# The first set of head tiles in a pool of its own, in a decoder kernel of twelve layers on one core

## The chip, the cores and the metric

The kernel runs on one core of a Trainium2 chip. A core has five engines that work side by side, each through a queue of its own: TensorE (PE, with its weight loads listed as PEld), VectorE (DVE), ScalarE (ACT), GpSimd (POOL) and SyncE (SP), which here only issues DMAs. The metric is the time of one execution on the device in microseconds. Before the change it was 1789.06 us, the median of three runs (1786.39, 1789.06 and 1797.75).

## The reference

The input `x` has 8 batches of 256 tokens of width 128, the context 8 batches of 512 tokens. Four decoder blocks follow, each with a self-attention, a cross-attention and a feed-forward layer, each added to `x` after a normalisation:

```python
x = x + _L0_attn_ref(_layernorm(x), ...)
...
x = x + _L1_attn_ref(_layernorm(x), ...)            # rotary, over the batch axis
x = x + _L1_xattn_ref(_layernorm(x), ctx_1024, ...) # one head
x = x + _L1_ffn_ref(_layernorm(x), ...)
x = x + _L2_attn_ref(_layernorm(x), ...)            # Fenwick mask, 16 heads
x = x + _L2_xattn_ref(_layernorm(x), ctx_1024, ...) # 16 heads
...
```

The layers around the change are the single-head cross-attention of block 1 and the two attentions of block 2:

```python
def _L1_xattn_ref(input_tensor, context, Wq, bq, Wk, bk, Wv, bv):
    q = jnp.einsum('bld,ed->ble', input_tensor, Wq) + bq
    k = jnp.einsum('bld,ed->ble', context, Wk) + bk
    v = jnp.einsum('bld,ed->ble', context, Wv) + bv
    scores = jnp.einsum('bqd,bkd->bqk', q, k) / q.shape[-1] ** 0.5
    return jnp.einsum('bqk,bkd->bqd', jax.nn.softmax(scores, axis=-1), v)
...
def _L2_xattn_ref(q, kv, ...):
    qh = (q @ Wq.T + bq).reshape(B, Lq, 16, 8)
    kh = (kv @ Wk.T + bk).reshape(B, Lkv, 16, 8)
    vh = (kv @ Wv.T + bv).reshape(B, Lkv, 16, 8)
    attn = jax.nn.softmax(jnp.einsum('bqhd,bkhd->bhqk', qh, kh) / 8 ** 0.5, axis=-1)
    return jnp.einsum('bhqk,bkhd->bqhd', attn, vh).reshape(B, Lq, 128) @ Wo.T + bo
```

The change leaves what is computed as it is.

## The kernel before

The activations stay in the core's memory throughout: `E.x` holds the 8 batches, `xt` their normalised transposes. The kernel falls into parts. First L0_attn and L0_xattn run woven together. Then the middle part (`_middle`, L1185) runs L0_ffn, L1_attn, L1_xattn, L1_ffn and L2_attn. Then come L2_xattn, L2_ffn and block 3.

**Head attention.** L0_xattn, L2_xattn, L3_attn and L3_xattn are computed by one function, `_heads_attention`, with tiles that the class `_Heads` (L345) holds in a pool named "hd". There are two sets of them, i = 0 and 1, used by turns: `mh_v` (2,672 B per partition), `mh_k` (16,384 B) and `mh_q` (16,384 B). Products of heads of width 8 use rows of `mh_k` and `mh_q` of which some must hold zeros and some ones, and `mh_v` has columns of ones, so each set is filled once before its first use. The function `fills` (L363) yields four copies per set on ScalarE, all by line L368 from a column of zeros or ones: the upper 64 rows of `mh_k`, two rows of `mh_k`, `mh_q`, and `mh_v`.

**When the tiles are made.** At the start of the kernel `_Heads` is made for L0_xattn. The middle part needs the space, so "hd" is closed before it (L1737) and `_Heads` is made anew towards its end: in `_middle`, after `scope.close()` (L1230), `E.beginning(then)` makes it through `heads()` (L1635), issues the first four fills, begins the layer (the bias row `mh_row` from `mh_bvt` and `mh_bps`), projects the keys and values of batch 0 (L422, L441) and starts to spread the keys by DMA. Then `fa(0, 1)` (L1237) runs the Fenwick attention over the first two batches (four half blocks, tiles `fa_`). The second `next(begun)` (L1239) projects the queries of batch 0 (`mh_qps`), spreads them by DMA (L438), and issues the remaining four fills, those of set 1. The rest of L2_attn and L1_ffn then run as a guest among the steps of L2_xattn.

**The layers before it.** `_middle` runs groups of two batches through L0_ffn (tiles `moe_`), the rotary L1_attn (`ra_`) and L1_xattn (`xa_`), staggered. At the end stand `ra(3)`, `xa(2)` and `xa(3)` (L1227 to L1229). L1_xattn ends in the additions of L1030. `ra` reads its projections from `ra_qkv` (24,576 B per partition); the products over it are those of L946 and L965, on VectorE and on GpSimd.

**Space.** Pools are stacks on a left and a right side of the memory. On the right side of the middle part lie, from the bottom: "moe" (two buffers of 4,096 B and two of 2,048 B per partition), "moe_c" (512 B), "ra1" (`ra_qkv`), then the smaller buffers of `ra_`, `xa_` and `rk_`. All are closed by `scope.close()`, after which the head pools are opened on the same side, from the bottom. A new pool's tile waits for those who last used the memory under it.

**Order.** The program is written out in full, and a scheduler that lays out the instructions of each engine may place one ahead of others that are written earlier, by the inputs that it expects to be ready. Steps of the head layers on TensorE keep their written order (`keep_in_program_order`, L459). Each engine then takes its instructions strictly as laid out. The lines that the prediction follows are these: L957 and L1008 (exponentials of `ra_` and `xa_`), L1025 (`xa_et`), L1117 (`fa_v`), L1131 (exponential of `fa_`), L1152 (`fa_ot`), L215 (`xt`) and L425 (`mh_kf`, `mh_qf`) on ScalarE; L1113 (`fa_kvps`) and L459 on TensorE.

Of the kernel before, what the change touches and what calls it, by code (L numbers as in the profile page):

```python
# [344 lines left out]
class _Heads:  # L345
# [4 lines left out]

    def __init__(self, E, ctx):
        self.E, nc = E, E.nc
        one = ctx.enter_context(E.tc.tile_pool(name="hd", bufs=1, side="right"))
        self.g = ctx.enter_context(E.tc.tile_pool(name="hd_g", bufs=2, space=PSUM, side="right"))
        self.one = one
        self.q, self.k, self.v = [], [], []
        for i in range(2):
            self.v.append(one.tile([P, SK // P, H * VW + 32 - VW], F32, name=f"mh_v{i}"))
            self.k.append(one.tile([P, H // 2, SK], F32R, name=f"mh_k{i}"))
            self.q.append(one.tile([P, H, S], F32R, name=f"mh_q{i}"))  # L360
        self.made = 0
# [1414 lines left out]
```

## Time and profile before

The profiled execution is one of the kernel on the chip. Its device time was 1792.07 us, of which 1790.2 lie between its first and last instruction.

| | before |
|---|---|
| median of three runs | 1789.06 us |
| profiled execution, device time | 1792.07 us |
| its span | 1790.2 us |
| mean granted TensorE clock | 0.917 |
| TensorE busy | 1475.6 us (82%) |
| VectorE busy | 1149.6 us (64%) |
| ScalarE busy | 882.0 us (49%) |
| GpSimd busy | 495.5 us (28%) |
| fills by L368 (8 long, of 3.60 us, for `mh_k`; 4 of 3.61 for `mh_q`; 4 of 0.76 for `mh_v`) | 14.4 + 14.4 + 14.4 + 3.1 us |

Eight of these sixteen fills are those of the start; the other eight lie between 862 and 894 us. Times in the timelines are counted from the span's start. A row of a timeline gives the start, the busy time, engine and line, the operation, the tile written and the tiles read, shapes, how many instructions were merged, and in brackets the idle time of the engine just before and what ended it. A share of busy time is an average over stages with different limits, so a stage is read by its own windows.

### The profile page before, as it was taken

Reading aid. Unit: us, or ns where it says so; the run is one execution under the profiler, and the core shown is the slowest. Engines: PE = TensorE matmul, PEld = TensorE weight load, DVE = VectorE, ACT = ScalarE, POOL = GpSimd, SP = SyncE. Lnnn points to the kernel's source line nnn. Section 1 sums busy time; section 2 is a strip of 40 time slices with the busy share of each in tenths; the row PEclk is TensorE's granted clock in tenths of the full one; section 3 lists DMA queues with packets and bytes.
Section 4 is the critical chain, followed back from the end, with each engine's and each line's share of the span. In section 5 each row is a group of like instructions: output and inputs, shape, how many; then the busy total and the mean of one; then the engine's idle time right before and its main releaser. Section 6 shows DMA issues by size and latency. Waiting matters only on the chain. (4 is left out here: it accounts for less than half of the span.)

```text
span 1790.2 us, 29309 instructions
## 1 busy us (share of the span) xinstructions
PE 1475.6 (82%) x10103; PEld 1066.1 (60%) x10141; DVE 1149.6 (64%) x3857; ACT 882.0 (49%) x1830; POOL 495.5 (28%) x987
## 2 busy tenths in 40 slices
PE   5689989999999989786558888878946799799986
PEld 3456677767655556554336666656615677677763
DVE  3567666765636676777457777668565666466656
ACT  7245455555642345322625656547643465455543
POOL 3122222222100121223323334332103433234422
PEclk8799999999999999897769999989965899899999
DMA  4011011104100000000111011111002221112100
GB/s 153 13 36 36 8 33 37 36 21 151 30 1 1 1 1 1 0 1 1 24 38 26 22 37 37 37 37 42 5 10 54 83 67 50 49 50 52 48 1 24
DMA packets 47236, 60.43 MB, mean 34 GB/s; under 512 B 5232, under 2 KB 36976, under 8 KB 46448
## 3 DMA queue, kind: packets, MB, share of 16 engines
q1 hardware_dynamic: 44720, 56.99, 12.0%
q8 instruction: 80, 1.31, 0.3%
q10 hardware_dynamic: 2368, 1.57, 0.3%
q14 instruction: 68, 0.56, 0.1%
HBM read 14.50 MB, written 1.05 MB: 9 GB/s over the span
## 5 line engine op out<-in xcount | busy, mean ns | idle before, releaser
L459 PE MATMUL mh_sps<-mh_k,mh_q 96*128 96x512 f32 (+2 forms) x1024 | 325.1, 400 | 53.2 <-DMA mh_q<-mh_qp 24.1
L459 PE MATMUL mh_bsps<-mh_q,mh_k 128*128 128x256 f32 (+1 forms) x1536 | 354.9, 337 | 7.0 <-ACT mh_e L595 4.1
L595 ACT ACTIVATE mh_e<-mh_bsps 128x512 f32<-128x512 f32 x512 | 281.0, 599 | 119.1 <-PE mh_bsps L459 111.9
L459 PEld LDWEIGHTS mh_bsps<-mh_q,mh_k 128*128 128x128 f32 x1536 | 267.8, 199 | 32.0 <-issue 6.9
L459 PEld LDWEIGHTS mh_sps<-mh_k,mh_q 96*128 96x128 f32 x1024 | 173.7, 204 | 101.0 <-issue 44.0
L522 DVE CUSTOM_DVE_ANT_0 mh_rest<-mh_sps,mask_b 128x512 bf16<-128x512 f32 x256 | 167.1, 684 | 81.2 <-PE mh_sps L459 78.0
L459 PE MATMUL mh_ops<-mh_e,mh_v 128*32 128x256 f32 (+1 forms) x3072 | 195.2, 375 | 1.3 <-DVE mh_nm L522 0.8
L541 DVE TENSOR_REDUCE mh_nm<-mh_sps 128x1 f32<-128x512 f32 x256 | 165.1, 680 | 33.8 <-PE mh_sps L459 33.6
L582 ACT ACTIVATE mh_e<-mh_bsps 128x384 f32<-128x384 f32 x256 | 118.7, 494 | 59.6 <-PE mh_bsps L459 36.2
L459 PEld LDWEIGHTS mh_ops<-mh_e,mh_v 128*32 128x32 f32 x3072 | 94.9, 112 | 67.0 <-issue 6.2
L197 POOL TENSOR_SCALAR ln_rstd<-ln_mv 128x2 f32<-128x2 f32 x96 | 22.0, 229 | 384.3 <-DVE ln_mv L195 384.0
L548 POOL CAST mh_hi<-mh_nm 128x8 fp32r<-128x8 f32 x128 | 25.0, 196 | 343.4 <-DVE mh_nm L522 211.1
L522 DVE CUSTOM_DVE_ANT_0 mh_rest<-mh_sps,causal 128x128 bf16<-128x128 f32 (+1 forms) x256 | 79.4, 352 | 50.5 <-PE mh_sps L459 48.4
L522 DVE CUSTOM_DVE_ANT_0 mh_rest<-mh_sps,km_q 128x128 bf16<-128x128 f32 (+1 forms) x256 | 79.4, 350 | 45.2 <-PE mh_sps L459 43.3
L215 ACT COPY xt<-ln_ps 128x256 f32<-128x256 f32 x96 | 36.0, 375 | 122.7 <-PE ln_ps L462 62.7
L560 ACT CAST mh_m<-mh_mps 8x256 fp32r<-8x256 f32 x128 | 46.2, 361 | 100.6 <-PE mh_mps L462 99.0
L885 ACT ACTIVATE moe_si<-moe_gps 128x512 f32<-128x512 f32 x64 | 38.0, 597 | 106.5 <-PE moe_gps L883 82.8
L628 ACT COPY mh_osb<-mh_ops 128x256 f32<-128x256 f32 x128 | 47.7, 372 | 84.2 <-PE mh_ops L459 84.0
L459 PE MATMUL mh_bsps<-mask_t,ident 128*128 128x512 bf16 x219 | 84.7, 387 | 0.4 <-ACT mh_e L595 0.4
L201 DVE TENSOR_SCALAR ln_z<-x,ln_mv,ln_rstd 128x128 f32<-128x128 f32 x136 | 44.3, 367 | 54.5 <-POOL ln_rstd L198 54.4
L883 PE MATMUL moe_ups<-xt,w_L_ffn 128*128 128x512 f32 x128 | 69.8, 628 | 6.9 <-ACT moe_si L885 4.8
L894 PEld LDWEIGHTS moe_dps<-w_L_ffn,moe_act 128*128 128x128 f32 x512 | 66.1, 204 | 15.7 <-issue 7.8
(360 smaller groups left out, 3089.5 us busy)
## 6 DMA issues: line engine op xcount, KB each, us to landing
mh_k<-mh_kp SPq DMA_DIRECT2D x64, 256.0 KB
mh_q<-mh_qp SPq DMA_DIRECT2D x256, 64.0 KB
mh_k<-mh_kp SPq DMA_DIRECT2D x64, 128.0 KB
w_L_ffn<-in_w_L_ffn SPq DMA_DIRECT2D x2, 1558.0 KB
w_L_attn<-in_w_L_attn SPq DMA_DIRECT2D x2, 1056.0 KB
ctx_t<-in_ctx_t SPq DMA_DIRECT2D x4, 512.0 KB
mh_q<-mh_m ACTq DMA_DIRECT2D x128, 8.0 KB
w_L_ffn<-in_w_L_ffn SPq DMA_DIRECT2D x2, 687.0 KB
```

What stands on the lines that cost most here:

```text
L201: (engine or nc.vector).tensor_scalar(z[:, q, :], E.x[:, 2 * b + q, :], mv[:, q, 0:1], rstd[:, q : q + 1], ALU.subtract, ALU.mult)
L215: E.nc.scalar.copy(E.xt(b), ps.rearrange("p q t -> p (q t)"))
L459: return self.E.tc.keep_in_program_order(self.E.nc.tensor.matmul(*a, **kw))
L522: nc.vector.tensor_tensor_reduce(rest[:, : scores.shape[1]], scores, lowered, -1.0, -FLOOR, ALU.add, ALU.min, accum_out=at)
L541: nc.vector.tensor_reduce(u.nm[:, c, col], ps, AX.X, ALU.max, negate=True)
L560: nc.scalar.copy(m, ps[:8].rearrange("p c q -> p (c q)"))
L582: nc.scalar.activation(e, ps, AF.Exp, scale=scale)
L595: nc.scalar.activation(e, ps, AF.Exp, scale=scale)
L628: nc.scalar.copy(osbs[b][:, u4 % 2, :], ops)
L883: nc.tensor.matmul(ps, W("w13")[:, o : o + P], xt, start=True, stop=True)
L885: nc.scalar.activation(si, pgate, AF.Silu)
L894: nc.tensor.matmul(ps[:, t, :], act[:, c, t * P : t * P + P], W("w2")[:, o : o + P], start=c == 0, stop=c == 1)
```

## The change

The first set of head tiles gets a pool of its own, "hd0", opened ahead of "hd" on the same side, so it takes the lowest 35,440 B per partition. The second set, and the tiles that `self.one` serves later (`mh_bvt`, `mh_row` and the buffers of the projections), stay in "hd", which now begins above.

```diff
     def __init__(self, E, ctx):
         self.E, nc = E, E.nc
+        zero = ctx.enter_context(E.tc.tile_pool(name="hd0", bufs=1, side="right"))
         one = ctx.enter_context(E.tc.tile_pool(name="hd", bufs=1, side="right"))
         self.g = ctx.enter_context(E.tc.tile_pool(name="hd_g", bufs=2, space=PSUM, side="right"))
         self.one = one
         self.q, self.k, self.v = [], [], []
-        for i in range(2):
+        for i, one in enumerate((zero, one)):
             self.v.append(one.tile([P, SK // P, H * VW + 32 - VW], F32, name=f"mh_v{i}"))
             self.k.append(one.tile([P, H // 2, SK], F32R, name=f"mh_k{i}"))
             self.q.append(one.tile([P, H, S], F32R, name=f"mh_q{i}"))
```

From L353 on, the lines of the changed kernel have numbers higher by one.

## The prediction

> **What bounds the kernel now.** I read the page first. TensorE is busy for 82% of a span of 1790.2 us, so time that the kernel loses lies in short stretches where TensorE waits. The chain of waits at the end of the page sits in the last layer and does not reach the change. So I went to the windows of 10 us around the end of the single-head cross-attention (tiles `xa_`) and the first half of the Fenwick attention (`fa_`), which lead into the head attention of L2_xattn (`mh_`).
>
> ```profile
> 840.00:850.00 10.00, 7.44 (x32) 5.33 (x31) 7.51 (x22) 4.08 (x11) 3.23 (x2) 0.84 0.00 0
> ...
> 860.00:870.00 10.00, 6.88 (x34) 5.33 (x32) 5.72 (x20) 7.61 (x5) 1.23 (x3) 0.89 0.00 0
> 870.00:880.00 10.00, 3.64 (x11) 2.88 (x11) 2.37 (x9) 9.96 (x11) 4.09 (x4) 0.62 0.27 70
> ...
> 900.00:910.00 10.00, 2.19 (x6) 1.10 (x6) 1.37 (x5) 0.85 (x2) 2.77 (x5) 0.50 0.12 30
> ```
>
> The columns are the stretch, its length, the busy time (and instructions) of TensorE, its weight loads, VectorE (DVE), ScalarE (ACT) and GpSimd, the granted clock of TensorE and the DMA's share and rate. From 870 to 880 us ScalarE is full, 9.96 of 10 us, while TensorE works 3.64 and VectorE 2.37. The timeline of ScalarE shows with what:
>
> ```profile
> 862.65 3.60 ACT L368 CAST mh_k<-plain 64x4096 fp32r<-64x4096 f32 x1 [2.35 <-DVE x L1030]
> 866.28 0.37 ACT L215 COPY xt<-ln_ps 128x256 f32<-128x256 f32 x1
> 866.66 3.60 ACT L368 CAST mh_k<-plain 2x4096 fp32r<-2x4096 f32 x1
> 870.27 3.60 ACT L368 CAST mh_q<-plain 128x4096 fp32r<-128x4096 f32 x1
> 873.78 0.74 ACT L368 COPY mh_v<-plain 128x668 f32<-128x668 f32 x1
> ...
> 876.27 0.35 ACT L1131 ACTIVATE fa_sc<-fa_sc 128x128 f32<-128x128 f32 x1
> ...
> 884.24 3.60 ACT L368 CAST mh_k<-plain 2x4096 fp32r<-2x4096 f32 x1
> 887.87 0.93 ACT L1117 COPY fa_v<-fa_kvps 128x256 f32<-128x256 f32 x3
> 888.66 3.63 ACT L368 CAST mh_q<-plain 128x4096 fp32r<-128x4096 f32 x1
> ```
>
> Four fills of the first set of head tiles, 3.60 + 3.60 + 3.60 + 0.74 = 11.5 us, wait for the last addition of the `xa_` layer (DVE L1030, 862.21 us). The work of `fa_` stands behind them. Its exponential (L1131) has its input at 870.62 us, when VectorE's L1130 ends, and starts at 876.27. Three of the second set's fills follow between later steps. TensorE's timeline shows who pays:
>
> ```profile
> 875.92 0.47 PE L1182 MATMUL fa_tps<-ident,fa_o 128*128 128x128 f32 x1 [8.39 <-ACT fa_v L1117]
> ...
> 892.89 0.79 PE L1155 MATMUL fa_yps<-w_L_attn,fa_ot 128*128 128x128 f32 x2 [3.79 <-ACT fa_ot L1152]
> ...
> 903.54 1.06 PE L459 MATMUL mh_qps<-xt,w_L_xattn 128*128 128x256 f32 x2
> 912.21 2.35 PE L459 MATMUL mh_sps<-mh_k,mh_q 96*128 96x512 f32 x4 [7.61 <-DMA mh_q<-mh_qp]
> ```
>
> TensorE waits 8.39 and 3.79 us for ScalarE. What then sets the start of the head attention (912.21) is batch 0's way through `fa_` to the query projection `mh_qps` at 903.54, and the spreading of the queries by DMA. The keys are not late: their DMAs are issued at 875.8.
>
> **The change part by part.** Sizes first. From the bottom of the right side lie the MoE buffers (2 x 4,096 + 2 x 2,048 B per partition), 512 B of gate weights and `ra_qkv` (24,576 B): 37,376 B. The new pool holds 2,672 + 16,384 + 16,384 = 35,440 B, so it ends inside `ra_qkv`. In the built order of the changed program its first fill waits for the two last products over `ra_qkv` (L965: VectorE's ends at 829.24 us, GpSimd's at 827.51), not for `xa_`. The second set still waits for the last L1030. No instruction is added or removed on any engine, SP's queue is the same throughout, and outside 825 to 905 us no engine's order changes.
>
> ScalarE's new order puts the first set's fills here: one ahead of two `xa_e`, one ahead of the copy of xt for batch 7, one ahead of another xt copy and `xa_q`, and the short one after `xa_k`. The second set moves up into the freed place, again with `fa_` work between. I walk that order forward from 825 us, each instruction starting when its engine is free and its inputs are there, with durations of the rows: fills 3.60, `xa_e` 0.69, `xa_et` 0.59, `fa_v` copies 0.37 (0.28 apart), a `fa_kvps` matmul 0.44 apart at full clock. The same walk over the old order brings `mh_qps` to 901.1 with matmuls at their shortest spacing and to 904.2 with spacings 1.4 times that; the trace has 903.54. So I carry both.
>
> *To the last addition of `xa_`.* Fill one runs 829.3 to 832.9, so the first `xa_e` slips from 831.6 to 832.9. Fill two runs 834.2 to 837.8: the xt copy slips from 835.7 to 837.8. Fill three runs 838.1 to 841.7: `xa_q` slips from 838.4 to 842.0. But `xa_k` slips only from 841.0 to 842.4, because the `fa_v` copies that stood before it now stand behind, and the second `xa_e` of that batch comes at 846.4 instead of 847.0. ScalarE was idle for 6.39 us before 831.59 and for 2.24 and 1.46 before the two copies; that is the cover. The last L1030 ends up 1.0 us earlier with short matmuls, 0.1 with long ones. If the cover fails, the 3.7 us of `xa_q` are lost.
>
> *From there to the exponential of the third half block.* Before: 876.27 - 862.21 = 14.1 us, four fills and 2.6 us of copies. After: 0.4 to start, a fill 3.6, xt copy 0.3, `mh_kf` and `mh_v` 1.0, two `fa_v` copies with their waits 1.1, a fill 3.6, two copies 0.6, and 0.2: 10.8 us. With long matmuls the `fa_v` copies wait longer, 12.65 (the old order gives 14.2 there). Gain 1.6 to 3.2. Of the 11.5 us of fills only 11.5 - 2 x 3.6 = 4.3 leave this stretch, since the second set moves in.
>
> *From there to `mh_qps`.* Before 903.54 - 876.27 = 27.3. There the second key fill (884.24) held the `fa_v` copies that free the banks of `fa_kvps`, and the query fill held the next exponential until 892.33. After, both fills lie while ScalarE waits for the normalised batch 0 (idle 3.17 before 883.57 now). The last `fa_kvps` follows 9.5 us after the exponential instead of 12.0, and the path is 24.3; with long matmuls 26.0 against 28.05 for the old order. Gain 2.0 to 3.1.
>
> Sum: 1.0 + 3.2 + 3.1 = 7.3 at best, 0.1 + 1.6 + 2.0 = 3.7 at worst. Granted clocks of 0.84 and 0.89 between 840 and 870 lie between the two; the trace's 903.54 is nearer the long matmuls. The middle is 5.5; I take 5. What is late next is the query DMA (905.61 to 912.21), which starts earlier by the same 5 and costs the same; all orders behind it are unchanged, so the 5 us stay.
>
> The clock is the open price. Rows: 0.50 in a window where TensorE worked 2.19 us, 0.62 at 3.64, and 0.89 at 6.88. The new order opens gaps of 2.1 and 2.0 us on TensorE (836.4 to 838.5 and 840.4 to 842.4). In the old order the matmuls up to 841 us ran slow already (`xa_kps` took 1.91 us at 839.09, where `mh_kps` of the same shape took 1.02 at 863.61). The new gaps could keep the next ones slow: two `xa_sps` 1.74, `xa_vps` 0.89 and `xa_tps` 0.44, or 3.1 us more. I count half of a microsecond of it in the 5, since the row of 840 to 850 (0.84) is nearer full clock than half. [...]
>
> **The rivals.**
> - All of the stall goes: 8.39 + 3.79 = 12.2 us. For it: these are the waits on TensorE. Against: the second set's fills move into the place. 1789.06 - 12.2 = 1776.9.
> - The gain is eaten: half clock after the new gaps costs 3.1, or the second set's fills hold the Fenwick block as the first did. Gain 0 to 2, taken as 1: 1788.
> - Slower: the three long fills delay `xa_q` by 3.7 us, the half clock adds 3.1, and the last L1030 comes 6.8 late, at 869.0; the later stretches return 3.6 to 6.3, the low end of which leaves 3.2 lost: 1792.3. It decides from a last L1030 between 865.8 and 868.5 on. Against it: `xa_k` slips only 1.4.
> - No fill moves, because the new pool waits for more than `ra_qkv`: 1789. Against it: the order and its waits.
>
> **How the numbers follow.** The profiled execution took 1792.07 (span 1790.2 and 1.87 around it), 3.0 above the median of 1789.06. 1792.07 - 5 = 1787.1 for such an execution, 1784.1 for the median. Chances: forecast (gain 3 to 8) 0.55, all of the stall 0.10, eaten 0.22, slower 0.10, no move 0.03. Range 1776 to 1793, from the full stall to the slower case; the three runs before spread from 1786.39 to 1797.75, so a median can sit a few us off by itself. 1% is 17.9 us, about what a measurement of this kernel can tell from no change, and no case reaches it: within 1% 0.95, faster 0.02, slower 0.03 for what I have not seen.
>
> **What would show it.** First fill at 829 to 830 us, and its four fills over by about 844. The `xa_e` behind it near 833. Last L1030 within 2 us of 862. One fill, not four, between it and `mh_kf`. TensorE's wait of 8.39 down to about 4 (for `fa_ot`). `mh_qps` near 898.5, and the same 8.7 us from it to `mh_sps`. I am wrong if the last L1030 passes 865.8, if the second set's fills stand in front of `fa_` exponentials for longer than 4 us, or if the granted clock between 835 and 850 falls under 0.7.

## The result and the profile after

The changed kernel took 1781.57 us (median of 11 runs, 1776.44 to 1788.22) against 1790.25 for the kernel before (11 runs beside them, 1786.39 to 1797.75). The medians lie 8.7 us apart. The ratio of the runs beside one another is 0.9956, 95% interval 0.9944 to 0.9967, or 7.9 us faster, between 5.9 and 10.0; that is less than 1%, and I go by it. The prediction said 5 us faster and a range of 1776 to 1793, so range and direction held and the gain was larger than said.

The profiled execution of after has a span of 1783.2 us and a mean granted clock of 0.921. Its times can't be laid over those of before as they stand. The copy of xt at 820.86 us, ahead of which both kernels have the same code, comes at 823.84. Over all twelve profiled executions of this study it lies between 816.1 and 824.6. So every time below is also given from that copy.

Windows of the changed kernel, with the columns of the prediction's first fence (stretch, length, busy time of TensorE, its weight loads, VectorE, ScalarE and GpSimd, granted clock, DMA):

```profile
840.00:850.00 10.00, 7.51 (x28) 4.50 (x29) 6.96 (x25) 9.61 (x17) 0.94 (x2) 0.77 0.00 1
...
860.00:870.00 10.00, 7.13 (x38) 5.28 (x36) 5.55 (x20) 7.43 (x7) 5.01 (x8) 1.00 0.10 25
870.00:880.00 10.00, 4.87 (x14) 3.63 (x15) 6.02 (x18) 7.34 (x9) 5.22 (x6) 0.60 0.35 80
...
890.00:900.00 10.00, 2.86 (x7) 1.48 (x7) 2.67 (x9) 1.11 (x3) 3.74 (x7) 0.50 0.00 0
```

ScalarE is now full between 840 and 850 (9.61 us) instead of between 870 and 880, where it fell from 9.96 to 7.34 while VectorE went from 2.37 to 6.02. ScalarE's timeline in the changed kernel shows where the fills went (all of L369):

```profile
832.30 3.60 ACT L369 CAST mh_k<-plain 64x4096 fp32r<-64x4096 f32 x1 [4.12 <-DVE ra_pv L966]
835.93 0.69 ACT L1009 ACTIVATE xa_e<-xa_sps,xa_nm 128x512 f32<-128x512 f32 x1
...
845.06 0.49 ACT L995 ACTIVATE xa_q<-xa_qps,w_L_xattn 128x256 f32<-128x256 f32 x1
845.43 0.70 ACT L999 ACTIVATE xa_k<-xa_kps,w_L_xattn 128x512 f32<-128x512 f32 x1
...
862.40 3.60 ACT L369 CAST mh_k<-plain 64x4096 fp32r<-64x4096 f32 x1 [3.15 <-DVE x L1031]
...
866.29 0.69 ACT L426 ACTIVATE mh_kf<-mh_kps,w_L_xattn 128x512 f32<-128x512 f32 x1
...
868.26 3.60 ACT L369 CAST mh_k<-plain 2x4096 fp32r<-2x4096 f32 x1
...
872.42 0.32 ACT L1132 ACTIVATE fa_sc<-fa_sc 128x128 f32<-128x128 f32 x1
```

The first fill starts when the rotary products end (`ra_pv`), as forecast. One fill stands between the last addition (`x` L1031) and `mh_kf`, where there were three long ones and a short one. TensorE's timeline in the changed kernel:

```profile
872.95 0.80 PE L1156 MATMUL fa_yps<-w_L_attn,fa_ot 128*128 128x128 f32 x2 [3.74 <-ACT fa_ot L1153]
...
893.11 0.48 PE L1183 MATMUL fa_tps<-ident,fa_o 128*128 128x128 f32 x1 [8.39 <-DVE fa_o L1149]
...
897.74 1.06 PE L460 MATMUL mh_qps<-xt,w_L_xattn 128*128 128x256 f32 x2
906.29 2.34 PE L460 MATMUL mh_sps<-mh_k,mh_q 96*128 96x512 f32 x4 [7.49 <-DMA mh_q<-mh_qp]
```

The wait of 8.39 for ScalarE is gone; the longest wait for ScalarE in this stretch is now 3.74, for `fa_ot`. A wait of 8.39 for VectorE's `fa_o` stands later, where before had 5.31 (at 899.00). The three stretches of the prediction, worked out from these rows and those of before:

| stretch | before | after | gain | predicted |
|---|---|---|---|---|
| xt copy to last addition | 862.21 - 820.86 = 41.35 | 861.96 - 823.84 = 38.12 | 3.23 | 0.1 to 1.0 |
| to the exponential of the third half block | 14.06 | 10.46 | 3.60 | 1.6 to 3.2 |
| to `mh_qps` | 27.27 | 25.32 | 1.95 | 2.0 to 3.1 |
| from `mh_qps` to `mh_sps` | 8.67 | 8.55 | 0.12 | 0 |

Together 8.9 us from the copy to the head attention. The spans differ by 7.0, since after came to the copy 2.98 later and took 1.08 less behind `mh_sps`. The first row is the one to explain: ScalarE does more work there than before, and yet the stretch got shorter.

### The profile page after: what moved, and what is told of

Same layout as the page of the kernel before. It is cut to its first block, busy times and chain, and to the rows that moved or that the text cites. A ratio compares the mean times of both kernels' runs of the same rounds, so it can differ in the third digit from the quotient of the medians.

```text
span 1783.2 us, 29345 instructions
## 1 busy us (share of the span) xinstructions
PE 1471.9 (83%) x10141; PEld 1064.4 (60%) x10141; DVE 1149.2 (64%) x3857; ACT 881.3 (49%) x1830; POOL 495.7 (28%) x987
## 5 line engine op out<-in xcount | busy, mean ns | idle before, releaser
L460 PE MATMUL mh_bsps<-mask_t,ident 128*128 128x512 bf16 x256 | 99.9, 390 | 0.4 <-ACT mh_e L596 0.4
```

The lines of the kernel that those rows point to most:

```text
L460: return self.E.tc.keep_in_program_order(self.E.nc.tensor.matmul(*a, **kw))
```

## The experiments

An edge `issue_after(i)` lays an instruction behind `i` in the order of the same engine; what else moves is the scheduler's answer to it. Ratios are to the kernel before, run beside each. The code shown leaves out the lines that only hand an instruction on or say for which set and layer the edit holds. The first four columns are from one profiled execution of each kernel: last addition counted from the xt copy, from there to the exponential of the third half block, from there to `mh_qps`, and the copy to `mh_sps`.

| kernel | last addition | to exponential | to `mh_qps` | copy to `mh_sps` | ratio (95%) |
|---|---|---|---|---|---|
| before | 41.35 | 14.06 | 27.27 | 91.35 | 1 |
| after | 38.12 | 10.46 | 25.32 | 82.45 | 0.9956 (0.9944 to 0.9967) |
| hold_before | 40.32 | 14.06 | 25.46 | 88.47 | 0.9987 (0.9972 to 1.0001) |
| hold_after | 38.14 | 11.81 | 18.77 | 77.36 | 0.9928 (0.9907 to 0.9950) |
| fa_behind | 40.12 | 22.04 | 19.94 | 90.79 | 1.0003 (0.9993 to 1.0013) |
| fills_late | 41.59 | 17.82 | 21.13 | 89.16 | 0.9987 (0.9972 to 1.0002) |
| rstd_first | 40.97 | 14.06 | 27.26 | 90.94 | 0.9989 (0.9977 to 1.0001) |
| products_last | 38.72 | 16.19 | 27.11 | 90.68 | 1.0006 (0.9995 to 1.0016) |
| add_first | 36.90 | 12.40 | 18.76 | 76.62 | 0.9931 (0.9908 to 0.9954) |
| one_less | 38.81 | 9.82 | 18.76 | 76.01 | 0.9934 (0.9916 to 0.9953) |
| one_more | 39.77 | 14.55 | 19.01 | 81.95 | 0.9968 (0.9949 to 0.9986) |
| all_in | 39.52 | 9.71 | 18.77 | 76.61 | 0.9915 (0.9902 to 0.9928) |

### The fills of the second set, on both kernels

Both kernels with this edit:

```diff
-            for f in fills[4:]:
-                f()
+            with tc.issue_after(E.heads.full.ins):   # the activation that makes mh_qf
+                for f in fills[4:]:
+                    f()
```

On the kernel before:

> The kernel before with the four fills of set 1 laid behind mh_qf, the activation of the queries of batch 0; set 0 waits for the xa_ layer as before. Theory 1 (each long fill of ScalarE that stands among the Fenwick steps costs its 3.6 us, or what is left of it after its cover): stretches up to the exponential of the third half block as before (last L1030 near 862, exponential 14 after it); from there to mh_qps 23 to 25.5 us instead of 27.3; the start of the head attention unchanged relative to mh_qps, since ScalarE idles for about 11 us there; total 2 to 4 us faster than before, 1786 to 1788. Rival (the fills only fill waits that DVE and GpSimd set anyway): that stretch stays at 27 to 27.5, total within 1 us of before.

Measured: the stretch to `mh_qps` took 25.46, within the theory's 23 to 25.5, and the head attention started 2.9 us earlier. The time is 2.3 us lower, but its interval (5.0 lower to 0.2 higher) just takes in no change. TensorE has the order of before in every instruction here, and yet the last addition came at 40.32 instead of 41.35; the granted clock between 850 and 860 was 0.96 in this execution and 0.84 in that of before. So that first number scatters by about 1 us.

On the changed kernel:

> The changed kernel with the four fills of set 1 laid behind mh_qf. Theory 1: the fill of 3.6 us after the last addition and the one before the exponential of the third half block are gone, so the exponential comes 4 to 7 us after the last L1031 instead of 10.5; from there to mh_qps 22 to 25 instead of 25.3; total 3.5 to 9 us faster than the changed kernel, 1773 to 1778. Rival (without the fills TensorE or VectorE bounds the Fenwick steps): 8.5 us or more after the last addition, 25 to mh_qps, total within 2 us of the changed kernel, 1780 to 1783. Last L1031 near 859 under both, since nothing ahead of it moves.

Measured: 1777.85 us, 12.9 faster than before and within the theory's total. By the two ratios it is some 5 us faster than the change alone; their intervals overlap a little (0.9944 to 0.9950), and in the profiled executions the head attention comes 5.1 us earlier. Its parts fell out otherwise: 11.81 to the exponential, where 4 to 7 was said, and 18.77 behind it, where 22 to 25 was said. TensorE's timeline of this kernel shows what sets the pace with the fills gone:

```profile
876.90 0.45 PE L1183 MATMUL fa_tps<-ident,fa_o 128*128 128x128 f32 x1 [3.86 <-DVE fa_o L1147]
...
884.30 0.45 PE L1183 MATMUL fa_tps<-ident,fa_o 128*128 128x128 f32 x1 [5.79 <-DVE fa_o L1149]
```

The long waits are now for VectorE and the GpSimd product ahead of it; the longest for ScalarE is 0.74. VectorE is busy for 7.57 of the 10 us from 860, and the exponential of the third half block is one of several things that it feeds there; that of the fourth follows 6.9 us later (877.01 - 870.13), not 14.2 (886.58 - 872.42 in after). The two stretches together are the safe reading: 30.6 us instead of 35.8.

### The same pools, without the move

```diff
-            for f in fills[:4]:
-                f()
+            with tc.issue_after(E.last_et.ins) if layer == "L2_xattn" else ExitStack():
+                for f in fills[:4]:
+                    f()
```

> The changed kernel with the four fills of set 0 laid on ScalarE behind the last xa_et, so the two pools and their addresses stay, and the move is taken out but for the 2 us by which the fills may start ahead of the last addition. Theory 1: fills from about 860, exponential of the third half block 12 to 14 us after the last L1031, total 1786 to 1790, like before. Rival (pools, addresses or the freed tiles of the second set matter, not the time of the fills): 1781 to 1783, like the changed kernel.

Measured: ratio 0.9987. The two pools and their addresses are those of the changed kernel, and 5.6 of its 7.9 us are gone; what is left is 2.3 (interval 0.4 slower to 5.0 faster). The fills start at 860.75, as soon as the last `xa_et` is over and 5.4 ahead of the addition (866.20), which no longer gates them. The exponential came 17.8 after the addition, not 12 to 14, because five long fills stand ahead of it here, two of them set 1's. So it is the time of the fills that pays, not the pools.

### Why the last addition came earlier

The first idea was TensorE's order, in which before has Fenwick steps between the `xa_ops`. In the kernel before, all of TensorE's Fenwick steps from the first `fa_tps` on were laid behind the last `xa_ops`:

```diff
+    def behind(op):
+        def issue(*a, **kw):
+            with E.tc.issue_after(E.last_ops.ins):
+                return op(*a, **kw)
+        return issue
+    ...
+        E.mm = behind(nc.tensor.matmul)
```

> The kernel before with TensorE's Fenwick steps from the first fa_tps on laid behind the last xa_ops; the fills stay behind the xa_ layer. Theory 2 (the 3.2 us that the changed kernel gains up to the last addition come from the order of TensorE, which had Fenwick steps between the xa_ops): last L1030 at 859 to 860.5 instead of 862.2, then as many us later in the Fenwick part; total 1787 to 1792. Rival (they come from the early fills themselves or from the granted clock): last L1030 at 861.5 to 863 and total 1789 to 1793.

Measured: last addition 40.12 after the copy, 1.2 earlier than in before and 0.2 earlier than in hold_before, which has the old order. By the clock of the trace it lies at 859.91, but the copy came 1.07 earlier too. The total is unchanged. The scheduler's answer also moved GpSimd: its second product then stood ahead of `ln_rstd`, which ended at 858.39. So the run does not weigh TensorE's order by itself, but that order alone, with no more gain than the scatter, does not account for 3.2 us. Next, the chain that ends in the last addition was read on all engines. The kernel before:

```profile
853.87 0.17 DVE L195 BATCH_NORM_AGGREGATE ln_mv<-ln_st 128x2 f32<-128x6 f32 x1
...
854.10 2.19 POOL L1136 TENSOR_TENSOR fa_v<-fa_v,fa_sc 128x1152 f32<-128x1152 f32 x1 [7.70 <-DVE ln_mv L195]
...
856.80 0.72 POOL L198 TENSOR_TENSOR ln_rstd<-ln_rstd,neg_half 128x2 f32<-128x2 f32 x1
...
857.47 1.27 POOL L1138 TENSOR_TENSOR fa_v<-fa_v 128x512 f32<-128x512 f32 x1
857.55 1.53 DVE L201 TENSOR_SCALAR ln_z<-x,ln_mv,ln_rstd 128x128 f32<-128x128 f32 x2 [0.38 <-POOL ln_rstd L198]
...
858.88 0.73 PE L214 MATMUL ln_ps<-ident,ln_z 128*128 128x128 f32 x2 [2.66 <-DVE ln_z L201]
...
860.26 1.92 PE L1028 MATMUL xa_ops<-xa_v,xa_et 128*128 128x128 f32 x8
```

The normalisation of batch 6 is ready for GpSimd at 854.04. GpSimd takes the Fenwick product first (2.19 us), so `ln_rstd` ends at 857.52, 3.5 us after the statistics, where the changed kernel takes 1.1. Then the two `ln_z` take 1.53 us beside the second product, and `ln_ps` waits 2.66 on TensorE with the last `xa_ops` behind it (its input `xa_et` was over by 856.47; it starts at 860.26). The changed kernel:

```profile
856.35 0.71 POOL L198 TENSOR_TENSOR ln_rstd<-ln_rstd,neg_half 128x2 f32<-128x2 f32 x1
857.09 0.60 DVE L201 TENSOR_SCALAR ln_z<-x,ln_mv,ln_rstd 128x128 f32<-128x128 f32 x2 [0.80 <-POOL ln_rstd L198]
...
857.50 0.33 PE L214 MATMUL ln_ps<-ident,ln_z 128*128 128x128 f32 x1 [0.55 <-DVE ln_z L201]
...
858.06 2.19 POOL L1137 TENSOR_TENSOR fa_v<-fa_v,fa_sc 128x1152 f32<-128x1152 f32 x1 [1.00 <-DVE fa_sc L1135]
...
859.14 1.16 PE L1029 MATMUL xa_ops<-xa_v,xa_et 128*128 128x128 f32 x8 [0.62 <-ACT xa_et L1026]
```

There the Fenwick steps come later, since the early fills stand ahead of their copies on ScalarE, and the product starts behind `ln_rstd` and `ln_z`: 34.2 us after the copy, against 33.2 in before, while the statistics of batch 6 (`ln_mv`) are ready at 32.1 and 33.2 (32.2 in hold_before). The two `ln_z` take 0.60. To test it, `ln_rstd` of batch 6 alone was put first on GpSimd in the kernel before:

```diff
-        nc.gpsimd.tensor_tensor(v4, v4, a.unsqueeze(3).to_broadcast([P, no, H, DH]), ALU.mult)
+        with E.tc.issue_after(E.single_rstd.ins) if t == 1 else ExitStack():
+            nc.gpsimd.tensor_tensor(v4, v4, a.unsqueeze(3).to_broadcast([P, no, H, DH]), ALU.mult)
```

> The kernel before with one edge on GpSimd: the product L1136 of the second half block (fa_v, 2.19 us) is laid behind ln_rstd of batch 6 (L198) instead of ahead of it; fills as before. New theory (the 3.2 us that the changed kernel gains up to the last addition come from GpSimd: ln_rstd stood behind that product, so ln_z and ln_ps came late, and the last xa_ops stood behind ln_ps on TensorE): ln_ps 2 us or more earlier, the wait of 2.66 for ln_z on TensorE under 0.8, last L1030 38 to 39.5 us after the xt copy near 821 (before 41.35, with the same code in another run 40.3), and from the addition on all as before: 2 to 3 us faster, 1787 to 1789. Rival (the early fills themselves, or the granted clock, bring the last addition forward): last L1030 40 us or more after that copy, total within 1 us of before.

Here `single_rstd` is the `ln_rstd` of batch 6. Measured: 40.97, so the theory in this form falls. The trace of this run shows why (the lines of the Fenwick part are one to three higher from here on):

```profile
850.18 2.18 POOL L1137 TENSOR_TENSOR fa_v<-fa_v,fa_sc 128x1152 f32<-128x1152 f32 x1
850.25 2.57 DVE L201 TENSOR_SCALAR ln_z<-x,ln_mv,ln_rstd 128x128 f32<-128x128 f32 x2 [0.77 <-POOL ln_rstd L198]
...
852.50 0.33 PE L214 MATMUL ln_ps<-ident,ln_z 128*128 128x128 f32 x1 [2.31 <-DVE ln_z L201]
...
855.33 1.72 PE L1028 MATMUL xa_ops<-xa_v,xa_et 128*128 128x128 f32 x8
```

`ln_rstd` is early (over at 850.21), but the product starts with its end, and now the two `ln_z` take 2.57 us: the transpose of the first starts at 852.50, 0.14 after the product's end (850.18 + 2.18 = 852.36). So the order on GpSimd's queue was only part of the cause. The next run differs from this one in the order of GpSimd and of VectorE behind `ln_z` alone (VectorE's Fenwick additions follow the products behind the last addition, which waits for TensorE in both runs, 1.02 and 1.03); both products are laid behind `ln_rstd` of batch 7:

```diff
-    E.single_rstd = E.rstd[6]
+    E.single_rstd = E.rstd[7]
```

> The kernel before, with GpSimd's two products of the second half block (L1136 and L1138) laid behind ln_rstd of batch 7; TensorE and ScalarE keep the order of the run with ln_rstd first, which gained nothing: there ln_z (VectorE, two of 0.3 us) took 2.57 us while GpSimd's 2.18 us product ran. Theory (VectorE's ln_z cannot run while GpSimd works on a long product; the early fills shift the Fenwick steps so that this product starts behind ln_z): both ln_z over within 0.7 us, ln_ps 35 to 35.5 us after the xt copy, last L1030 38 to 39 after it instead of 41; total 1 to 3 us faster than before, 1788 to 1790, since the second half block's output then comes later but under the fills. Rival (the last addition depends on something else, such as the granted clock): ln_z over in 0.7 but last L1030 at 40 or more; or ln_z still over 1.5.

```profile
855.57 0.71 DVE L201 TENSOR_SCALAR ln_z<-x,ln_mv,ln_rstd 128x128 f32<-128x128 f32 x2
...
856.08 0.33 PE L214 MATMUL ln_ps<-ident,ln_z 128*128 128x128 f32 x1
...
857.91 1.16 PE L1028 MATMUL xa_ops<-xa_v,xa_et 128*128 128x128 f32 x8
...
861.28 2.19 POOL L1137 TENSOR_TENSOR fa_v<-fa_v,fa_sc 128x1152 f32<-128x1152 f32 x1
861.35 3.54 DVE L201 TENSOR_SCALAR ln_z<-x,ln_mv,ln_rstd 128x128 f32<-128x128 f32 x2 [0.52 <-POOL ln_rstd L198]
863.54 1.26 POOL L1139 TENSOR_TENSOR fa_v<-fa_v 128x512 f32<-128x512 f32 x1
863.60 0.33 PE L214 MATMUL ln_ps<-ident,ln_z 128*128 128x128 f32 x1 [2.32 <-DVE ln_z L201]
...
864.94 0.33 PE L214 MATMUL ln_ps<-ident,ln_z 128*128 128x128 f32 x1 [1.01 <-DVE ln_z L201]
...
865.31 0.37 ACT L215 COPY xt<-ln_ps 128x256 f32<-128x256 f32 x1 [2.16 <-PE ln_ps L214]
```

Here the two `ln_z` of batch 6 take 0.71, `ln_ps` starts 35.7 after the copy (35 to 35.5 was said), and the last addition comes at 38.72, within 38 to 39. This is where the 2 to 3 us of the first stretch lie: what counts is that no long GpSimd product runs ahead of `ln_rstd` or beside `ln_z`.

The pace of TensorE's matmuls has a part in it. In before TensorE stands 2.66 us for `ln_z`; behind that its granted clock is 0.50 (858.9 to 860.9), and the last `xa_ops` takes 1.92 us. In rstd_first it stands 2.31 us, and the last `xa_ops` takes 1.72. In the changed kernel, where the wait for `ln_z` is 0.55, the clock is 1.00 from 850 to 870 and the last `xa_ops` takes 1.16, as it does in products_last, which doesn't wait there. Of the 2.25 us between rstd_first and products_last, 0.7 is the earlier `ln_ps`; most of the rest is the slower matmuls behind it (four `fa_kvps` 1.92 instead of 1.03, `xa_ops` 1.72 instead of 1.16). The last `xa_ops` is as long in hold_before, fills_late and one_more (1.91, 1.92 and 2.00 us), which wait 2.66, 2.38 and 2.40 us for `ln_z`. That the wait lowers the clock is my reading and is not shown: no run sets the clock by itself, and in hold_before an `xa_ops` right behind a wait of 2.74 us (849.68) took 1.16.

The total did not follow (1.0006). The same trace says where the gain went: the products now run beside the `ln_z` of batch 7, which take 3.54, and ScalarE's xt copy, laid ahead of the second fill, waits 2.16 for it. The exponential comes 16.19 after the addition instead of 14.06, so 2.1 of the 2.6 us are given back there.

In the changed kernel VectorE still loses time ahead of the last addition, which stands behind a Fenwick addition that waits 2.90 for GpSimd (L1145, 861.62). Laid behind it, on top of hold_after:

```diff
+        with E.tc.issue_after(E.last_add.ins) if t == 1 else ExitStack():
             nc.vector.tensor_tensor(v[:, :2, :], v[:, :2, :], v[:, 2:4, :], ALU.add)
```

> The changed kernel with set 1's fills behind mh_qf, and with VectorE's L1145 of the second half block (which waits for GpSimd's fa_v) laid behind the last addition L1031 instead of ahead of it. If VectorE's queue holds the last addition as the trace of the changed kernel reads (2.90 of waiting ahead of it, its xa_ops over by 860.1): last L1031 about 1.5 us earlier, 36.5 to 37 us after the xt copy instead of 38.1; total 0 to 1.5 us faster than with the fills alone behind mh_qf (which took 1777.85), since the last addition no longer gates a fill. Rival (the Fenwick path, which now starts behind the addition, is the longer one): same total or up to 1 us slower.

Measured: the addition at 36.90, as expected, the head attention 0.7 earlier, and a time that can't be told from hold_after. With the fills gone, the last addition no longer gates the path.

### How much cover the early fills had

Once with a fill less, once with a fill more, both on top of hold_after and both for the first set of block 2 alone. For the fill less, `plain` gets a third column (number 2) with ones in two rows and zeros elsewhere:

```diff
-            yield lambda k=k: fill(k[64:, :, :], 0)
-            yield lambda k=k: fill(k[TOP : TOP + 2, :, :], 1)
+            yield lambda k=k: fill(k[64:, :, :], 2)
```

> As the kernel with set 1's fills behind mh_qf, but set 0 of block 2 is filled with one long copy less: rows 64 to 127 of mh_k from one column that holds the zeros and the two ones. ScalarE has 3.6 us less ahead of xa_q, but the scheduler's order changes with it. Theory of the prediction (early fills have cover and cost almost nothing): last L1031 within 1 us of 38.1 after the xt copy unless ln_rstd falls behind a fa_v product on GpSimd again; total 1775 to 1780. Rival (early fills cost their length): last L1031 at 35 to 36, total 1774 to 1776.

```diff
-            yield lambda q=q: fill(q, 0)
+            yield lambda q=q: (fill(q, 0), fill(q, 0))
```

> As the kernel with set 1's fills behind mh_qf, but mh_q of set 0 is filled twice, the second time behind xa_k where the short fill stood: 3.6 us more of ScalarE ahead of the second xa_e. Theory of the prediction (cover ends about here): ScalarE had 0.35 us to spare ahead of that xa_e, so it slips by about 3 us, the last L1031 with it, 40.5 to 41.5 after the xt copy, and the total by 2 to 3.3, 1780 to 1781. Rival (hidden): total within 1 us of 1777.85.

Measured: with one less, the last addition stays (38.81 against 38.14) although `xa_q` came 2.3 us earlier. The head attention came 1.4 earlier in the profiled execution, but the time can't be told from hold_after (1781.19 us, where 1775 to 1780 was said). With one more, the next `xa_e` slipped by 1.35 us, the last addition by 1.6 (2.4 to 3.4 was said; 0.8 of it is the last `xa_ops`, which took 2.00 instead of 1.16), the head attention by 4.6. The ratio rose from 0.9928 to 0.9968, 7 us, more than was said, though the two intervals just touch. Three early long fills are thus about what the idle time of ScalarE holds: the third costs at most the 1.4, a fourth cost 4.6 up to the head attention. Why that is more than its 3.6 stays open.

### A version that beats both

The changed kernel with set 1's fills behind `mh_qf`, the Fenwick addition behind the last one, and the single key fill in both sets:

> The changed kernel with set 1's fills behind mh_qf, VectorE's L1145 of the second half block behind the last addition, and rows 64 to 127 of mh_k filled by one long copy in both sets. By the single runs: head attention 1 to 2 us earlier than with the fills alone behind mh_qf (77.4 us from the xt copy near 821 to mh_sps), 75.3 to 76.5; total 1775.5 to 1777.5 if that lasts. Rival (no further gain, since the query DMA and the Fenwick path set the start): 76.5 or more, total 1777 to 1779.

Measured: 1775.38 us (median of five runs), 15.2 us faster than before (12.9 to 17.5). Its interval (0.9902 to 0.9928) lies wholly below that of the change alone (0.9944 to 0.9967). From the copy to `mh_sps` it took 76.6, at the edge of the rival, so its lead over hold_after isn't shown.

## Why the prediction was right, and where it was short

- *The fills move, and their start.* Right: 829.3 when counted as in before (832.30 less the 2.98), four fills over by 844.1, `xa_e` at 832.95 (835.93 less the 2.98). `xa_q` slipped by 3.7 and `xa_k` by 1.4, both as walked, and the last `xa_e` came 0.8 earlier where 0.6 was said.
- *"The last L1030 ends up 1.0 us earlier with short matmuls, 0.1 with long ones."* This is the term that was mis-sized: 3.2 measured, 2.2 against the 40.32 of hold_before. The walk held up to the last `xa_e`. Behind it, it missed that the delayed Fenwick steps also take GpSimd's product away from `ln_rstd` and `ln_z`, and with it TensorE's wait of 2.66 and the long last `xa_ops` behind that wait (1.92 at a granted clock of 0.50, against 1.16 at 1.00 in the changed kernel). The two runs on GpSimd's order showed it: 40.97 with the product beside `ln_z`, 38.72 without.
- *To the exponential: 1.6 to 3.2.* 3.60 measured, a little above. The stretch of 10.46 fits the walk with short matmuls (10.8); the long ones (12.65), towards which the prediction leaned, did not occur: the granted clock was 1.00 from 850 to 870.
- *To `mh_qps`: 2.0 to 3.1.* 1.95, just under the low end, at granted clocks of 0.60 from 870 to 880 and 0.50 from 890 to 900. By the prediction's own figures, 27.3 less 24.3 is 3.0 and not 3.1, and 14.1 less 10.8 is 3.3 and not 3.2; neither changes the forecast. That the set 1 fills still cost there was right: hold_after took 5 us more off both stretches.
- *The clock after the new gaps.* 0.77 between 840 and 850, above the 0.7 that was named, and no delay that shows behind it: `xa_kps` took 1.91 in both kernels, the four `xa_sps` 1.99 instead of 1.88, and the last `xa_e` was early. The half microsecond was not needed here. No run shows by itself that a gap lowers the clock. What was measured is that in five of these executions the last `xa_ops`, behind a wait of 2.3 to 2.7 us for `ln_z`, took 0.6 to 0.8 us longer than its 1.16; in before the granted clock there was 0.50.
- *"What is late next is the query DMA ... and costs the same."* Right: 8.55 instead of 8.67, and 8.55 to 8.69 in all runs.
- *The rivals.* All of the stall would have been 1776.9; two of the long fills and their 3.74 us of wait stayed in the place, as the argument against it said. The slower case had its first sign (`xa_q` late by 3.7) but not its deciding one: the last addition came at 861.96, not past 865.8. That the gain is eaten, or that nothing moves, is ruled out by the interval.

So the sum was short mainly by its first term. That term was an accident of order: no part of the change aims at GpSimd. The three terms add up to 8.8, above the best case of 7.3, and each lies outside its own range; that the time still fell within the forecast's gain of 3 to 8 is partly luck.

## What to carry to other kernels

When a walk along one engine's new order gives a small gain, look also at which long instructions of the other engines now run ahead of or beside the short ones on the path: here that stretch gained 2.2 to 3.2 us, nearly as much as the 3.6 of the stall that the change was made for. Work that only prepares buffers belongs where its engine idles, and the whole of it counts: moving the first set alone left some 5 us to be had from the second. Before two traces are compared, count from an event ahead of which both run the same code, since here that event moved by over 8 us between executions.

## What was unexpected on the hardware

The two short `ln_z` of VectorE took longer beside a long GpSimd product, and the trace books this as busy time, not as a wait. In the changed kernel, ahead of the product, they took 0.60 us; beside products they took 1.53 in before, 2.57 in rstd_first and 3.54 in products_last. In products_last the two transposes behind them start at 863.60 and 864.94, 0.13 and 0.14 us after the two products end (861.28 + 2.19 = 863.47 and 863.54 + 1.26 = 864.80). Not every VectorE instruction got longer: in before, `fa_q` (L1102, which reads a matmul's output) took 0.28 at 854.13 beside the 2.19 us product (0.29 in products_last at 855.16, without one), and in after `ln_st` (L194, which reads `x`) took 0.29 at 858.21 beside the product from 858.06 to 860.25 (0.29 in products_last at 859.49, without one). No run shows what sets `ln_z` apart from these two.
